# A two-layer graph network: GpSimd's gathers of layer 1's edges moved behind layer 0's scatters of tokens

## The chip, the core and the metric

The kernel runs on one core of a Trainium2 chip. The core has five engines with a queue each: TensorE (PE; its weight loads are shown as PEld), VectorE (DVE), ScalarE (ACT), GpSimd (POOL) and SyncE (SP). They run side by side and meet in semaphores. DMAs are issued from the queues of SP, ACT and POOL; the indirect ones, whose addresses come from a tile in SBUF, all from POOL. The metric is the time of one execution on the device in microseconds (us), as a median of several.

## The reference

Nodes: 3125 with 256 features; edges: 100,000, sorted by destination, each with one of 8 types. Two layers, each made of a graph part, an attention part and a mixture of experts:

```python
edge_index = jnp.stack([src, dst])
xn = _layernorm(x, axis=-1)
x = x + _L0_gnn_ref(xn, edge_index, ...) + _L0_mix_ref(xn[None], ...)[0]
x = x + _L0_ffn_ref(_layernorm(x, axis=-1)[None], ...)[0]      # 8 experts, top 2, hidden 1024, exact GELU
xn = _layernorm(x, axis=-1)
x = x + _L1_gnn_ref(xn, ..., edge_index, edge_type_8) + _L1_mix_ref(xn[None], ...)[0]
x = x + _L1_ffn_ref(_layernorm(x, axis=-1)[None], ...)[0]      # 6 experts, top 2
```

`_L0_gnn_ref` sums the neighbours of each node twice, with a linear layer, a norm and a SiLU after each sum. `_L0_ffn_ref` sends each node (a token) to the two of its 8 experts with the highest router probability. `_L1_gnn_ref` is an attention over the edges: a score for each edge from its source, destination and type, a softmax over the edges of a destination, and a weighted sum of the source rows.

## The kernel before, in words

128 partitions; the nodes stand in 25 blocks (NB) of 128. The stages, in order of time:

1. Layer 0's graph part builds a dense matrix of edge counts (adj) and sums neighbours as matrix products (L2183), twice. The second pass runs over groups of node columns, `GROUPS1`: five of 512, two of 256 and one of 128. After each group `Routes.tokens` works out, on VectorE, the router's choice for its blocks and where each token goes (`slot`, L1905), and POOL scatters the tokens, one indirect DMA for each block and each of the two choices (L1909, 50 in all), into the DRAM tensor `route_x`, sorted by expert. Then `Routes.plan` works out which tiles of which experts are left to do.
2. `Blocks` prepares layer 1's edges: the edges, sorted by destination, are cut into 25 blocks of 128 runs, with 34 edges a run (15 in the last block). Its constructor issues 75 indirect gathers on POOL (L1048): for each of dst, src and type, and each block, 128 runs of 34 whole numbers (136 bytes). `Blocks.finish` is a generator with the arithmetic on them, in pieces.
3. `Routes.results` works out from which row each token's result will come back, and writes it over `slot` (L1971); so it waits for the scatters that read the old `slot`.
4. `experts` runs 32 steps: 8 with the first 256 tokens of each expert, then 24 as the plan says. A step: SP loads its tokens `fx` from `route_x` (L1993), its weights (two of 1 MB, L2002 and L2004) and small rows; TensorE transposes the tokens (L2013), VectorE scales them into `fxe` (L2015); 8 times, a product of `fxe` with a part of the first weights goes to `fhp` (L2030, two buffers in PSUM) and ScalarE's GELU brings it to `fhid` (L2031); then 16 products with the second weights (L2038) give `fyp`, VectorE adds a row (L2040), and ACT's queue stores it (L2041). The next step's transposes stand between a step's fhp and fyp. After each step `beside(s)` is called: from step 8 on it advances `Blocks.finish` by a piece (the first reads `b_dst`, L1061), at step 16 POOL loads layer 1's weights `wn` (L2244, 8 DMAs), at step 22 `score_weights` multiplies them (L2064).
5. Layer 1: results are gathered back (L2300), the table of source rows is made (L2319), and for each block the rows of its edges are gathered by POOL (L1383, 831 gathers of 128 rows) and reduced by TensorE (L1468), with the attention's softmax, the six experts and small products for the scores (L1214, L1415, L1429) woven in.

The order of the work: outside the parts named next a scheduler places the instructions on each queue, by readiness and priority. In `with tc.manual_schedule(engines=ORDERED)` around `experts`, PE, DVE and ACT keep the order in which the code names the instructions; POOL and SP do not. A POOL instruction placed early in the queue is executed early, and what stands behind it waits. In the queue that was built, the 75 gathers and the 50 scatters are interleaved at the end: 44 scatters, 14 gathers of b_dst, 4 scatters, 11 gathers of b_dst, 6 of b_src, 2 scatters, 19 of b_src, 25 of b_rel (the types), 8 loads of wn. The first gather waits for a VectorE instruction of the second pass (L2195) and for counts of TensorE and ScalarE; each POOL DMA also waits for the one eight places before it.

Of the kernel before, what the change touches and what calls it, by code (L numbers as in the profile page):

```python
# [9 lines left out]
I32 = mybir.dt.int32  # L10
# [7 lines left out]
P = 128  # L18
# [390 lines left out]
def run_all(steps):  # L409
    for _ in steps:  # L410
        pass
# [493 lines left out]
BO = [sum(BW[:b]) for b in range(NB + 1)]  # L905
# [124 lines left out]
class Blocks:  # L1030
# [3 lines left out]
    def __init__(self, nc, keep, dram, pool, a, places):  # L1034
        k = lambda shape, dt, name: keep.tile(shape, dt, name=name)
        t = lambda shape, dt, name: pool.tile(shape, dt, name=name)
        n = BO[NB]
        self.at = k([P, n], I32, "b_at")
        self.dl = k([P, n], F32, "b_dl")
        self.rel = k([P, n], BF, "b_rel")  # L1040
        self.found = k([P, 1], F32, "b_found")
        self.order = dram.tile([n, P], BF, name="b_order")
        self.raw = raw = {}
        for name, src in (("dst", "dst"), ("src", "src"), ("rel", "edge_type_8")):
            raw[name] = t([P, n], I32, "b_" + name)
            flat = a[src].rearrange("(e o) -> e o", o=1)
            for b in range(NB):
                nc.gpsimd.indirect_dma_start(  # L1048
                    out=raw[name][:, BO[b]:BO[b + 1]], out_offset=None, in_=flat,
                    in_offset=bass.IndirectOffsetOnAxis(ap=places.blocks[:, b:b + 1], axis=0))  # L1050

    def finish(self, nc, C, dram, pool, ps):

# [81 lines left out]
class Layer1:  # L1135
# [50 lines left out]
    def load(self, A, c):  # L1186

        if c >= A["n"]:
            return
        k = min(CW, A["w"] - c * CW)  # L1190
        i = A["c0"] + c * CW
        oe = self.wk.tile([P, CW * P], BF, name="oe", bufs=3)
        self.nc.sync.dma_start(oe[:, :k * P], self.B.order[i:i + k, :].rearrange("c e -> (c e)")[None, :]
                               .to_broadcast([P, k * P]))
        A["oe"][c] = oe
# [849 lines left out]
def score_weights(nc, C, a, late, f, wn, blk_p):  # L2045

    at_w = f.tile([P, 2, 2 * HD], F32, name="at_w")
    head = f.tile([P, 2, HD], F32, name="head")
    for oc in range(2):
        nc.vector.tensor_scalar(head[:, oc, :], C.row[:, :HD], float(-4 * oc), C.pd[DH],  # L2050
                                op0=OP.add, op1=OP.is_equal)
    for i, name in enumerate(("L1_gnn_attn_srcc", "L1_gnn_attn_dstc")):
        col = f.tile([P, 2], F32, name=f"att{i}")
        nc.sync.dma_start(col, a[name])
        for oc in range(2):
            nc.vector.tensor_scalar(at_w[:, oc, i * HD:(i + 1) * HD], head[:, oc, :],
                                    col[:, oc:oc + 1], None, op0=OP.mult)

    score_w = late.tile([P, 2, 2 * R * HD], F32, name="score_w")
    sp = blk_p.tile([P, 2, R, 2 * HD], F32, name="sp", tag="w")  # L2060
    for r in range(R):
        for k in range(2):
            for oc in range(2):
                nc.tensor.matmul(sp[:, k, r, :], wn[:, r, oc, k * P:(k + 1) * P], at_w[:, oc, :],  # L2064
                                 start=(oc == 0), stop=(oc == 1))
    for k in range(2):
        nc.vector.tensor_copy(score_w[:, k, :R * HD].rearrange("p (r h) -> p r h", r=R),
                              sp[:, k, :, :HD])
        nc.vector.tensor_copy(score_w[:, k, R * HD:].rearrange("p (h r) -> p r h", r=R),
                              sp[:, k, :, HD:])  # L2070
    return score_w
# [3 lines left out]
def fast(ctx: ExitStack, tc: tile.TileContext, a, out, flag):  # L2075
    nc = tc.nc
# [28 lines left out]
    with tc.tile_pool(name="a_sb", bufs=1) as a_sb, tc.tile_pool(name="a_ps", bufs=2, space=PSUM) as a_ps, \  # L2105
# [3 lines left out]
        with tc.tile_pool(name="find", bufs=1) as find:  # L2109
            places = Places(nc, C, keep, find, a_ps, a)  # L2110
# [34 lines left out]
    with tc.tile_pool(name="g", bufs=1) as g1, tc.tile_pool(name="ga", bufs=4) as ga, \  # L2145
# [12 lines left out]
        for layer, parts in enumerate((px, py)):  # L2158
# [5 lines left out]
            for c, cw in (GROUPS if layer == 0 else GROUPS1):  # L2164
# [3 lines left out]
                for kb in range(NB // KB):  # L2168
# [9 lines left out]
                    for i in range(KB):  # L2178
                        k = k0 + i
                        n = P if k < NB - 1 else LAST  # L2180
# [31 lines left out]
                for i in range(nt):  # L2212
                    t = c // P + i
# [18 lines left out]
    with tc.tile_pool(name="blk", bufs=1) as blk, tc.tile_pool(name="blk_p", bufs=1, space=PSUM) as blk_p, \  # L2232
            tc.tile_pool(name="f", bufs=1) as f:
        B_ = Blocks(nc, late, dram, blk, a, places)

        score_w = None
        wn = f.tile([P, R, 2, D], F32, name="wn")
        steps = B_.finish(nc, C, dram, blk, blk_p)

        def beside(s):  # L2240
            nonlocal score_w
            if s == 16:
                for r in range(R):
                    nc.gpsimd.dma_start(wn[:, r], a["L1_gnn_W"][r].rearrange("(k p) n -> p k n", p=P))  # L2244
            if s == 22:
                score_w = score_weights(nc, C, a, late, f, wn, blk_p)
            if s >= 8:
                next(steps, None)
            if s < NE0 + NT - 1:
                return  # L2250
            run_all(steps)

            ok = blk.tile([P, 1], F32, name="ok")
            nc.vector.memset(ok, 1.0)
            tot = blk_p.tile([1, 1], F32, name="tot", tag="w")
            nc.tensor.matmul(tot, found_w, ok, start=True, stop=False)
            nc.tensor.matmul(tot, B_.found, ok, start=False, stop=True)
            nc.vector.tensor_scalar(flag, tot, float(2 * E), None, op0=OP.not_equal)

        T_.results(nc, C, blk)  # L2260
        with tc.tile_pool(name="fw", bufs=2) as fw, tc.tile_pool(name="fk", bufs=3) as fk, \
                tc.tile_pool(name="fp", bufs=2, space=PSUM) as fp:
            with tc.manual_schedule(engines=ORDERED):
                experts(tc, C, T_, a, f, fw, fk, fp, beside)


    with tc.tile_pool(name="n1", bufs=1) as n1:
# [7 lines left out]
        with tc.tile_pool(name="r", bufs=1) as r1, tc.tile_pool(name="rw", bufs=3) as rw, \  # L2275
# [21 lines left out]
            for t in range(NB):  # L2297
                for i in range(2):
                    y = rw.tile([P, D], F32, name=f"y{i}")
                    nc.gpsimd.indirect_dma_start(  # L2300
                        out=y, out_offset=None, in_=T_.y,
                        in_offset=bass.IndirectOffsetOnAxis(ap=T_.back[:, i * NB + t:i * NB + t + 1], axis=0))
# [22 lines left out]
                ap = rp.tile([P, 2 * R * HD], F32, name="ap", tag="b")  # L2325
# [8 lines left out]
                n = P if t < NB - 1 else LAST  # L2334
# [34 lines left out]
@with_exitstack  # L2369
def gps_two_layers(ctx: ExitStack, tc: tile.TileContext, a, out):  # L2370
    nc = tc.nc
    hold = ctx.enter_context(tc.tile_pool(name="hold", bufs=1))
    flag = hold.tile([1, 1], I32, name="flag")
    fast(tc, a, out, flag)
    with tc.If(nc.values_load(flag[0:1, 0:1], min_val=0, max_val=1) > 0):
        general(tc, a, out)
# [51 lines left out]
```

## Time and profile before

| | us |
|---|---|
| median of 3 runs | 3694.38 (3680.18 to 3694.63) |
| the profiled execution | 3702.6 |
| its span, first to last instruction | 3700.7 |
| first scatter of tokens (L1909) | 739.9 |
| first gather of b_dst (L1048) | 939.7 |
| last scatter of tokens, start | 985.8 |
| last gather of b_rel, start | 1041.5 |
| first fhp of the experts (L2030) | 1015.4 |
| end of the experts' last fyp | 1526.7 |
| first gather of results for layer 1 (L2300) | 1530.2 |

Busy over the whole span: PE 2658.4 us (72%), DVE 1753.3 (47%), ACT 735.2 (20%), POOL 1057.7 (29%). These shares are averages over stages with different limits, and say little of the stretch around the change. Between 950 and 1053 us PE was busy for 15.40 us, DVE 13.46, ACT 5.53 and POOL 76.37; between 1053 and 1500 us, in the experts' steps, PE for 445.04 of 447.

Such a profile is read from the end: the chain of waits follows the work that ended last back to what released it, step by step; "issue" in it is time in which an engine waited for nothing that the profile shows, and "remote" or "another core or an unknown queue" time whose releaser was not found. The timeline lists the instructions of each engine with the idle time before each.

### The profile page before, as it was taken

The page shows a single profiled execution, that of the slowest core. Times are in us where ns is not written, and L with a number is a line of the kernel's source. Part 1 is how long each engine was busy: PE and PEld are TensorE (multiplying, and loading weights), DVE is VectorE, ACT ScalarE, POOL GpSimd, SP SyncE. Part 2 cuts the span into 40 slices and gives each one's busy share as a digit, 9 for nine tenths or more (in the row PEclk, how much of TensorE's full clock was granted, in tenths as well). Part 3 has the DMA queues.
Part 4 walks back from the last instruction along what each step waited for, and adds up shares of the span by engine and source line. Part 5 has one row for each costly group of instructions (what it writes and reads, how often), then busy time and mean ns, then how long its engine had stood idle before and what let it go on. Part 6 is the DMA issues. An engine that isn't in the chain of part 4 may idle for free.

```text
span 3700.7 us, 38218 instructions
## 1 busy us (share of the span) xinstructions
PE 2658.4 (72%) x13696; PEld 1789.8 (48%) x13696; DVE 1753.3 (47%) x3882; ACT 735.2 (20%) x1637; POOL 1057.7 (29%) x1040
## 2 busy tenths in 40 slices
PE   2787999999179999799634527736655755755778
PEld 1565544546158888544323424534443543543456
DVE  6888533556301111376415545445454453554552
ACT  3344111212112222232100001102101111201122
POOL 1000000021620000320233554553554554554410
PEclk9899999999589999899867767877876877977899
DMA  8533222332346665553423332432342343343322
GB/s 298 152 79 74 84 77 66 89 118 72 86 132 192 192 197 161 152 158 122 138 78 85 96 108 78 116 113 78 104 121 82 98 120 92 98 121 91 96 65 81
DMA packets 382414, 421.68 MB, mean 114 GB/s; under 512 B 143878, under 2 KB 316044, under 8 KB 381958
## 3 DMA queue, kind: packets, MB, share of 16 engines
q1 hardware_dynamic: 311680, 270.61, 24.2%
q0 software_dynamic: 49072, 132.49, 12.8%
q10 hardware_dynamic: 21462, 16.03, 1.4%
q8 instruction: 110, 1.80, 0.2%
q14 instruction: 90, 0.74, 0.1%
HBM read 321.04 MB, written 97.96 MB: 113 GB/s over the span
## 4 chain that ended last, share of the span: by engine, by line
PE 55%; another core or an unknown queue 19%; DVE 14%; issue 4%; DMA 3%; ACT 2%; POOL 2%; ACTq 1%; SPq 0%; POOLq 0%; DVEq 0%
PE agg L2183 11%; PE fhp L2030 6%; PE fyp L2038 6%; PE sums L1468 6%; PE hp L1270 5%; PE hp L2319 4%; PE yp L1322 3%; DVE r L1454 2%; PE hp L2203 1%; DVE oh_a L1619 1%; DVE oh_s L1619 1%; PE kv L1727 1%; PE cnt L1634 1%; PE kvp L2337 1%
## 5 line engine op out<-in xcount | busy, mean ns | idle before, releaser
L1383 POOL DMA_INDIRECT r<-tab,b_at x831 | 863.2, 1039 | 1063.0 <-PE tp L1524 482.5
L1468 PE MATMUL sums<-r,oh 128*128 128x264 f32 x1662 | 435.7, 419 | 74.3 <-DVE oh L1457 55.8
L1214 PE MATMUL dp<-a,ot 128*128 128x64 bf16 x2493 | 116.6, 210 | 482.7 <-DVE own L1225 318.7
L1468 PEld LDWEIGHTS sums<-r,oh 128*128 128x128 f32 x1662 | 343.1, 209 | 161.6 <-issue 60.1
L1214 PEld LDWEIGHTS <-ot 128*128 128x128 bf16 x2493 | 108.6, 109 | 511.0 <-issue 398.6
L1909 POOL DMA_INDIRECT route_x<-x,slot x50 | 50.4, 1007 | 829.3 <-DVE slot L1905 678.2
L2030 PE MATMUL fhp<-fxe,fw 128*128 128x256 f32 x1024 | 238.7, 391 | 46.0 <-issue 20.6
L1225 DVE TENSOR_TENSOR own<-dp,orel 128x512 f32<-128x512 f32 (+1 forms) x122 | 74.1, 607 | 404.0 <-remote 313.1
L1454 DVE TENSOR_TENSOR r<-r 128x1792 f32<-128x1792 f32 (+2 forms) x123 | 240.5, 1955 | 0.0
L2183 PE MATMUL agg<-at,px 128*128 128x512 bf16 (+2 forms) x1050 | 237.5, 357 | 2.2 <-DMA row_g<-in_L_gnn_g 2.2
L1322 PE MATMUL yp<-ew,h 128*128 128x256 f32 x600 | 168.7, 433 | 95.9 <-DVE xs L1326 91.9
L2030 PEld LDWEIGHTS fhp<-fxe,fw 128*128 128x128 f32 x1024 | 189.3, 194 | 89.1 <-issue 23.6
L1273 ACT ACTIVATE h<-hp,bc 128x512 f32<-128x512 f32 (+2 forms) x168 | 105.2, 639 | 631.3 <-PE hp L1270 324.3
L2038 PE MATMUL fyp<-fw,fhid 128*128 128x256 f32 x1024 | 227.8, 381 | 0.0
L2183 PE MATMUL agg<-at,py 128*128 128x512 bf16 (+4 forms) x1200 | 218.7, 335 | 1.5 <-issue 1.5
L2038 PEld LDWEIGHTS fyp<-fw,fhid 128*128 128x128 f32 x1024 | 193.3, 191 | 25.3
L2300 POOL DMA_INDIRECT y<-route_y,slot x50 | 49.8, 996 | 510.6 <-DMA wq<-in_L_mix_wqT 481.8
L2319 PE MATMUL hp<-wt,xt 128*128 128x512 f32 x400 | 186.9, 615 | 11.7 <-ACT xt L345 3.1
L1322 PEld LDWEIGHTS yp<-ew,h 128*128 128x128 f32 x600 | 125.2, 218 | 133.4 <-DVE xs L1326 101.2
L2031 ACT ACTIVATE fhid<-fhp,fb 128x256 f32<-128x256 f32 x256 | 121.3, 474 | 323.2 <-PE fhp L2030 280.0
L1270 PE MATMUL hp<-xt,ew 128*128 128x512 f32 (+2 forms) x336 | 170.3, 629 | 19.2 <-ACT h L1273 12.2
L1270 PE MATMUL hp<-h,ew 128*128 128x512 f32 (+2 forms) x336 | 155.8, 590 | 2.1 <-issue 2.0
(418 smaller groups left out, 3810.5 us busy)
## 6 DMA issues: line engine op xcount, KB each, us to landing
fw<-in_L_ffn_W SPq DMA_DIRECT2D x64, 1024.0 KB
ew<-in_L_ffn_expert_w SPq DMA_DIRECT2D x126, 256.0 KB
at<-adj SPq DMA_DIRECT2D x44, 640.0 KB
route_x<-zero SPq DMA_DIRECT2D x104, 256.0 KB
tab<-stage SPq DMA_DIRECT2D x25, 1056.0 KB
oe<-b_order SPq DMA_DIRECT2D x97, 256.0 KB
adj<-adj_o SPq DMA_DIRECT2D x78, 250.0 KB
r<-tab,b_at POOLq DMA_INDIRECT x831
```

Source lines behind the costliest of these rows:

```text
L1214: nc.tensor.matmul(dp[:, i, :, :].rearrange("p h r -> p (h r)"), ot[:, i * P:(i + 1) * P], A["a3"][:, j, :], start=(j == 0), stop=(j == 2))
L1270: nc.tensor.matmul(hp[:, :W], ws[i, e][:, n, j * P:(j + 1) * P], x[:, n, :W], start=(n == 0), stop=(n == 1))
L1273: nc.scalar.activation(o[:, j, :W], hp[:, :W], AF.Relu, bias=b[:, e, j:j + 1])
L1322: nc.tensor.matmul(yp, h2[e][:, n, i * P:(i + 1) * P], ws[3, e][:, n, :], start=(n == 0), stop=(n == 1))
L1383: st = self.nc.gpsimd.indirect_dma_start(out=r[:, c, :], out_offset=None, in_=self.table, in_offset=bass.IndirectOffsetOnAxis(ap=self.B.at ...
L1454: nc.vector.tensor_tensor(rv, rv, r[:, :k, D:, None].to_broadcast([P, k, HD, DH]), OP.mult)
L1468: mm = nc.tensor.matmul(self.sums, oh[:, c, :], r[:, c, :], start=(i == 0), stop=(i == w - 1))
L2030: nc.tensor.matmul(hp, w1[:, k, i * P:(i + 1) * P], xe[:, k, :], start=(k == 0), stop=(k == 1))
L2031: nc.scalar.activation(hid[:, i, :], hp, AF.Gelu, bias=b1[:, 0, i:i + 1])
L2038: nc.tensor.matmul(yp, hid[:, i, t * P:(t + 1) * P], w2[:, i, :], start=(i == 0), stop=(i == K1 - 1))
L2183: nc.tensor.matmul(agg[g][:, :cw], parts[j][:n, k, g * P:(g + 1) * P], at[:n, i, :cw], start=(k == 0 and j == 0), stop=(k == NB - 1 and j ...
L2319: nc.tensor.matmul(hp.rearrange("p r d -> p (r d)"), xt[:, k, :], wt[:, k, j * 512:(j + 1) * 512], start=(k == 0), stop=(k == 1))
```

## The change

The gathers leave the constructor of `Blocks` and become a generator, `load`, that issues them five at a time under `keep_in_program_order`; `beside` advances it by two pieces after each of the steps 0 to 7. The loads of `wn` get `keep_in_program_order` too. The first pieces are thus named in the code after the scatters, and after the experts' step 0. `keep_in_program_order` fixes where an instruction stands in its queue; it adds no wait for another engine.

```diff
-        self.raw = raw = {}
+        self.raw = {name: t([P, n], I32, "b_" + name) for name in ("dst", "src", "rel")}
+        self.places = places
+
+    def load(self, tc, a):
+
         for name, src in (("dst", "dst"), ("src", "src"), ("rel", "edge_type_8")):
-            raw[name] = t([P, n], I32, "b_" + name)
             flat = a[src].rearrange("(e o) -> e o", o=1)
             for b in range(NB):
-                nc.gpsimd.indirect_dma_start(
-                    out=raw[name][:, BO[b]:BO[b + 1]], out_offset=None, in_=flat,
-                    in_offset=bass.IndirectOffsetOnAxis(ap=places.blocks[:, b:b + 1], axis=0))
+                tc.keep_in_program_order(tc.nc.gpsimd.indirect_dma_start(
+                    out=self.raw[name][:, BO[b]:BO[b + 1]], out_offset=None, in_=flat,
+                    in_offset=bass.IndirectOffsetOnAxis(ap=self.places.blocks[:, b:b + 1], axis=0)))
+                if b % 5 == 4:
+                    yield
...
+        loads = B_.load(tc, a)
         steps = B_.finish(nc, C, dram, blk, blk_p)
...
             if s == 16:
                 for r in range(R):
-                    nc.gpsimd.dma_start(wn[:, r], a["L1_gnn_W"][r].rearrange("(k p) n -> p k n", p=P))
+                    tc.keep_in_program_order(nc.gpsimd.dma_start(
+                        wn[:, r], a["L1_gnn_W"][r].rearrange("(k p) n -> p k n", p=P)))
...
-            if s >= 8:
+            if s < 8:
+                for _ in range(2):
+                    next(loads, None)
+            else:
                 next(steps, None)
```

In the queue that is built from it POOL has the 50 scatters, then the 25 gathers of b_dst, 25 of b_src, 25 of b_rel, then the 8 loads of wn. The other queues keep their order.

## The prediction

> **What bounds the kernel now.** I read the chain of waits first, for the stretch from the last aggregation of layer 0 to the second step of the experts (columns: start, length, what).
>
> ```profile
> 939.70 0.99 POOL b_dst L1048
> ...
> 956.25 0.94 POOL b_dst L1048
> 957.50 1.00 POOL route_x L1909
> ...
> 985.83 1.57 POOL route_x L1909
> 987.70 0.99 POOL b_src L1048
> ...
> 1010.26 2.25 DMA b_src<-in_src,bstart_i
> 1013.41 1.93 DVE fxe L2015
> 1015.38 1.22 PE fhp L2030 x2
> ...
> 1024.94 10.01 issue
> 1035.43 10.03 issue
> 1045.93 7.22 another core or an unknown queue
> ```
>
> From 939.70 to 1010 the end hangs on GpSimd's gathers. Thirty-one of them (14, then 11 and 6) stand ahead of the last six scatters of tokens, and the experts cannot load a token before the last scatter has landed. From 1024.94 on the chain shows something else: waits of ten microseconds that nothing in the profile explains.
>
> The timeline gives the two costs of the queue (the bracket is the idle time before the instruction and what ended it).
>
> ```profile
> 947.55 0.16 DVE L1905 CAST slot<-route_at 128x2 int32<-128x2 f32 x1
> 957.50 1.00 POOL L1909 DMA_INDIRECT route_x<-x,slot  x1 [0.30 <-issue]
> 978.25 0.15 DVE L1905 CAST slot<-route_at 128x1 int32<-128x1 f32 x1 [1.22 <-DVE pl_ci L1924]
> 985.83 1.57 POOL L1909 DMA_INDIRECT route_x<-x,slot  x1 [0.31 <-issue]
> 991.78 4.37 SPq L1993 DMA_DIRECT2D fx<-route_x  x4
> ```
>
> The slots of the seventh group are ready at 947.55 and its first scatter goes at 957.50: ten microseconds of pure queue. The last slots come at 978.25. Their VectorE chain is not long; it has become slow.
>
> The same view of ScalarE shows what slows it, with a normal step of the experts and a place in layer 1 beside it.
>
> ```profile
> 1020.06 0.85 ACT L2031 ACTIVATE fhid<-fhp,fb 128x256 f32<-128x256 f32 x2
> 1024.47 0.47 ACT L2031 ACTIVATE fhid<-fhp,fb 128x256 f32<-128x256 f32 x1 [3.56 <-PE fhp L2030]
> 1034.95 0.47 ACT L2031 ACTIVATE fhid<-fhp,fb 128x256 f32<-128x256 f32 x1 [10.01 <-issue]
> 1045.45 0.47 ACT L2031 ACTIVATE fhid<-fhp,fb 128x256 f32<-128x256 f32 x1 [10.03 <-issue]
> 1053.17 0.84 ACT L2031 ACTIVATE fhid<-fhp,fb 128x256 f32<-128x256 f32 x2 [7.24 <-remote]
> ...
> 1111.59 0.47 ACT L2031 ACTIVATE fhid<-fhp,fb 128x256 f32<-128x256 f32 x1 [0.39 <-PE fhp L2030]
> ```
> ```profile
> 2064.63 0.36 ACT L1417 COPY ls<-lp 8x256 f32<-8x256 f32 x1 [21.54 <-remote]
> 2091.40 0.17 ACT L1430 COPY sc<-cp 128x8 f32<-128x8 f32 x1 [26.41 <-remote]
> ```
>
> A GELU (L2031) normally follows its matmuls after 0.39 us; here it waits 10, although the matmuls before it ended at 1023.2 and 1026.1. In layer 1 the matmuls of cp (L1429) end at 2066.5 and ScalarE takes them at 2091.40. Both stand in an unbroken run of GpSimd's indirect DMAs: 939.70 to 1048.33 (with the eight loads of wn at its end), and 2041.0 to 2087.0. Both end 4 to 5 us after the run. So I read: **while GpSimd issues indirect DMAs without a pause, hand-overs between engines become late, those from TensorE worst, until about 4.8 us after the run.** The VectorE chain from 954.63 is the milder form: steps that took 0.2 us before it take 0.7 to 1.4.
>
> **The change, part by part.** *Removed from the front of the queue:* 31 gathers at 1.25 us (start to start, 939.70 to 975.19 for the b_dst). *Added:* no instruction. In the built program's GpSimd queue the 50 scatters now come first, then 75 gathers in one row, then the eight loads of wn. The gathers wait only for the DMA eight places before them and, once, for TensorE and ScalarE counts passed long ago: nothing ties a piece to its step. TensorE, VectorE, ScalarE and SP keep their order; only the lane that SP's first fx load waits for, and two of VectorE's waits on lanes, change.
>
> *When the last scatter goes.* With four scatters from 947.7 to 952.8 the queue then pauses. The VectorE chain stands at 954.63; six dependent steps of 0.2 us bring own (L1892) to 955.9. In the seventh group own to the second cast took 3.3 us (944.95 to 948.26), here one token block less: 3.0, so 959, with the first cast 0.7 earlier. Two scatters at 1.28 end at 960.6, against 987.4: **26.8 us earlier**.
>
> *When the experts start.* Scatter end to fx load 4.4 us (987.4 to 991.78): 965.0. Load to transposes 2.9 (994.66): 967.9. Transposes 1.1, fxe 1.0, to the first fhp 1.4 (1013.94 to 1015.38): 971.4. To the first GELU 4.7 (1020.06): **976.1, or 44 us earlier**. Before, fxe also stood behind the plan's slot cast (L1971, 1012.55); its chain of some 22 small steps starts here at 957.4 in an unslowed VectorE, and at 0.2 to 0.6 us each is done by 967, under the load.
>
> [...]
>
> *What is moved, and when it ends.* The run now starts at 960.9: 75 times 1.25 is 93.8, to 1054.7; the loads of wn took 5.9 (1042.45 to 1048.33), to 1060.5; plus 4.8 (1048.33 to 1053.17): engines are free again at **1065.3, not 1053.17: 12.1 us later**. Who needs these data is far off: b_dst at 1180.5 (L1061, step 8), wn at 1382.6 (L2064); GpSimd's next work is at 1530. This is covered by over 100 us; uncovered, VectorE would hold up fxe by the same amount.
>
> *The stretch between,* 976.1 to 1065.3, is 89 us inside the run; the trace has only 33 us of such a stretch (1020.06 to 1053.17), five GELUs long. By its rows: two GELUs at once, the third after 4.4, then one in 10.5. That gives the eighth GELU of step 0 at 980.5 + 5 x 10.5 = 1033.0. fyp starts 0.6 later and takes 8.4: 1042. The next fhp ends at 1043, two GELUs at 10.5 come by 1064, the third and fourth at 1065.3 and 1066.2. In the present trace step 1's fourth GELU starts at 1068.58. So **the gain is 2.4 us**. If the first 20 us of a run are clean (in layer 1 the first late hand-over comes at 2060, 19 us after 2041.0), GELUs three and four come by 978.5, 12.5 us sooner, and step 1's fifth comes with the release against 1069.45: a gain of 3.3. I take 3.
>
> Bounds of this unknown. *No late hand-over at all:* eighth GELU at 976.1 + 7 x 0.87 (1110.73 to 1111.59) = 982.2 against 1055.81: 73.6 us gained. *Stuck until the release, as at 2066:* two more GELUs at 1065.3, four at 0.87, the eighth at 1069.2 against 1055.81: 13.4 us lost.
>
> [...]
>
> The sum: 3702.6 (span 3700.7 and 1.9 around it) minus 3 is 3699.6; the profiled execution lies 8.2 above the median 3694.38, which gives **3691**.
>
> **Rivals.** *The brake is weak on the experts* (0.20). VectorE's hand-overs inside the run cost about 1.2 us; if TensorE's cost that, a GELU takes 0.87 + 1.2, a step 8 x 2.07 + 6.9 = 23.5. In 89 us that is 3.8 steps where now one is done: 2.8 x 14.35 (fhp at 1065.00 and 1079.35) is 40 gained, 3654. For: the hand-overs at 967.4 and 1020 were prompt. Against: all four after 1022, and layer 1. *No brake* (0.07): 3621; no long run in the trace speaks for it. *Stuck* (0.18): place, step 0's GELUs; price 13.4 (3708); it decides when fewer than six of them pass before the run ends, for then the later release is not paid back. For: 2066 to 2091. Against: the present gathers, of 136 bytes a row, let one through in 10.5. That the pieces do not run beside the steps, as the change says, is part of the forecast.
>
> **How the numbers follow.** The forecast has 0.55; its own range is 3680 to 3705, the spread of the runs (14 us) about it. To hold 0.8 the range takes in the stuck case whole and the upper half of the weak one: 3649 to 3708. No change, within 0.5% (18.5 us, about what a measurement of this kernel can tell), is most of the forecast, the stuck case where nothing lengthens it, and the near edge of the weak one: 0.62. Faster: weak and free, and a little of the forecast: 0.28. Slower: stuck with a run that is itself longer beside the experts' 2 MB of weights a step: 0.10.
>
> **What would show it.** The last scatter at about 959 and the first fhp at 971; 75 gathers without a gap to 1055; release at 1065; between, GELUs with idle times of 10 us and 10 to 14 of them in all; full steps of 14.35 afterwards, and layer 1 unchanged. I am wrong if GELUs run at under 3 us apiece inside the run, if the gathers stretch beyond 1070, or if the last scatter still waits past 970.

## The result, and the profile after

| | before | after |
|---|---|---|
| median of 21 runs, us | 3691.22 (3667.04 to 3709.52) | 3691.08 (3675.86 to 3705.59) |
| the profiled execution | 3702.6 | 3687.65 |
| its span | 3700.7 | 3685.6 |
| last scatter of tokens, end | 987.4 | 960.1 |
| first GELU of the experts | 1020.06 | 972.50 |
| end of the wn loads, and of GpSimd's run | 1048.33 | 1059.78 |
| step 1's eighth GELU | 1072.04 | 1074.74 |
| first gather of results, after the experts | 1530.16 | 1529.56 |

The ratio after to before is 1.0008 (95% interval 0.9992 to 1.0023): no difference. The two profiled executions differ by 15 us, but the experts end 0.6 us apart; the rest lies in layer 1, whose code is the same (2170.5 us from the first gather of results to the end before, 2156.0 after; a second profile of the kernel after has 2166.1). The profile of after runs 2.25 us ahead of that of before already at the seventh group's own (942.70 against 944.95), for reasons that lie before the change; where it matters this is said below. Lines of after are 5 higher than those of before up to the experts, 6 at wn, 10 from the gathers of results on; the gathers of edges, L1048 before, are L1051.

The chain of waits of after, for the stretch that was shown of before (start, length, what):

```profile
958.27 6.01 DMA route_x<-x,slot
...
965.03 2.96 DMA fx<-route_x
...
969.45 46.25 another core or an unknown queue
...
1016.72 43.78 another core or an unknown queue
1060.53 0.42 DVE fy L2045
1060.95 4.62 another core or an unknown queue
1065.58 0.41 DVE fy L2045
1066.01 0.43 ACTq L2046
1066.54 0.48 ACT fhid L2036
```

The gathers are gone from the front of the chain: from the last scatter it goes straight to the first load of tokens. In their place stand three waits without a known releaser, 94.7 us together, up to 1065.58. The timeline shows what they are (in brackets the idle time before an instruction and what ended it).

```profile
956.40 0.15 DVE L1910 CAST slot<-route_at 128x1 int32<-128x1 f32 x1
958.27 1.84 POOL L1914 DMA_INDIRECT route_x<-x,slot  x1 [0.30 <-DVE pl_ex L1945]
1052.95 0.95 POOL L1051 DMA_INDIRECT b_rel<-in_edge_type,bstart_i  x1 [0.30 <-issue]
1053.89 5.89 POOL L2250 DMA_DIRECT2D wn<-in_L_gnn_W  x8
964.30 1.62 SPq L1998 DMA_DIRECT2D fx<-route_x  x3
972.50 0.84 ACT L2036 ACTIVATE fhid<-fhp,fb 128x256 f32<-128x256 f32 x2
974.20 0.47 ACT L2036 ACTIVATE fhid<-fhp,fb 128x256 f32<-128x256 f32 x1 [0.86 <-issue]
...
984.92 0.47 ACT L2036 ACTIVATE fhid<-fhp,fb 128x256 f32<-128x256 f32 x1 [4.43 <-remote]
987.32 1.06 PE L2018 MATMUL ftp<-ident,fx 128*128 128x128 f32 x4
993.33 0.48 ACT L2036 ACTIVATE fhid<-fhp,fb 128x256 f32<-128x256 f32 x1 [7.93 <-remote]
1004.52 0.47 ACT L2036 ACTIVATE fhid<-fhp,fb 128x256 f32<-128x256 f32 x1 [10.72 <-remote]
1066.01 0.43 ACTq L2046 DMA_DIRECT2D route_y<-fy  x1
1066.54 0.84 ACT L2036 ACTIVATE fhid<-fhp,fb 128x256 f32<-128x256 f32 x2 [61.54 <-DVE fy L2045]
...
1005.05 5.98 PE L2043 MATMUL fyp<-fw,fhid 128*128 128x256 f32 x15 [10.50 <-issue]
1039.51 0.58 PE L2035 MATMUL fhp<-fxe,fw 128*128 128x256 f32 x1 [2.22 <-issue]
1067.07 7.64 PE L2035 MATMUL fhp<-fxe,fw 128*128 128x256 f32 x24 [26.98 <-ACT fhid L2036]
1015.73 0.99 DVE L2020 TENSOR_SCALAR fxe<-ftp,flng,flnb 128x256 f32<-128x256 f32 x2 [46.27 <-remote]
1060.53 0.42 DVE L2045 TENSOR_TENSOR fy<-fyp,fb 128x256 f32<-128x256 f32 x1 [43.80 <-remote]
```

Read it by engine. GpSimd issues 75 gathers without a gap from 960.42 to 1053.9, and wn to 1059.78. ScalarE's GELUs start promptly, then fall behind: 4, 8, 11 us. The eighth of step 0 passes at 1004.52. VectorE's next work, fxe of step 1, comes at 1015.73, 27 us after the transposes (ftp) that it reads ended at 988.38. TensorE has made the first half of fyp, 16 of its 32 matmuls, by 1011 at the latest. VectorE takes it at 1060.53, **some 50 us late**, the last 43.8 of them idle; the chain has 0.02 us between the signal that it waited for and its start, so what came late is the signal, and not VectorE. ScalarE's queue stands behind the store of that fy, and TensorE, which has crept through eight single matmuls of step 1, waits for ScalarE from 1040.1 on. Everything goes on between 1065.6 and 1066.5, some 6 us after GpSimd's last DMA was issued.

Not only what waits for another engine is slow. Those eight matmuls start 2.1 to 2.8 us apart, each after idle time in which TensorE waited for nothing that the profile shows ("issue"); at full pace a matmul of that line takes 0.22 us (before has 32 in 7.16 us from 1064.84).

Layer 1 has the same two rows as before, with 18.54 us of idle time for ls (21.54 before) and 26.33 for sc (26.41), in its run of gathers:

```profile
2059.86 0.36 ACT L1422 COPY ls<-lp 8x256 f32<-8x256 f32 x1 [18.54 <-remote]
2086.55 0.17 ACT L1435 COPY sc<-cp 128x8 f32<-128x8 f32 x1 [26.33 <-remote]
```

Idle time is not all lateness: the matmuls that ls reads ended at 2057.1, 2.7 us before it; those of sc at 2061.7, 24.9 us before it.

### The profile page after: what moved, and what is told of

It reads as the page before. It is cut to its first block, busy times and chain, and to the rows that moved or that the text cites. A ratio compares the mean times of both kernels' runs of the same rounds, so it can differ in the third digit from the quotient of the medians.

```text
span 3685.6 us, 38218 instructions
## 1 busy us (share of the span) xinstructions
PE 2660.9 (72%) x13696; PEld 1791.3 (49%) x13696; DVE 1750.9 (48%) x3882; ACT 734.8 (20%) x1637; POOL 1052.7 (29%) x1040
## 4 chain that ended last, share of the span: by engine, by line
PE 51%; another core or an unknown queue 21%; DVE 16%; issue 5%; DMA 3%; ACT 2%; POOL 1%; SPq 1%; ACTq 0%; DVEq 0%; POOLq 0%
PE agg L2188 10%; PE fhp L2035 6%; PE fyp L2043 6%; PE sums L1473 5%; PE hp L1275 4%; PE hp L2329 4%; PE yp L1327 3%; DVE r L1459 2%; PE hp L2208 1%; DVE oh L1462 1%; DVE oh_a L1624 1%; DVE oh_s L1624 1%; PE cnt L1639 1%; PE kv L1732 1%
```

## The experiments

The theory (T): an unbroken run of GpSimd's gathers holds up hand-overs between engines (the signal of one engine that another waits for) until it ends; the change brings the experts forward, gives the run to their first steps, and ends it later. Rivals: the experts start slowly by themselves (R1); the DMA engines' bandwidth is shared (R2); each gather costs its share wherever it stands (R3). Times below are medians beside runs of the kernel before on the same chip. This turned out to matter: on the four chips on which the experiments ran, the kernel before took 3685.82 (e1 to e4), 3116.69 (e5 to e8), 3692.58 (e9, e10) and 3118.68 us (e11, e12).

### Tying the pieces to their steps: e1_tied

```diff
+                if b % 5 == 0:
+                    at = self.pool.tile([P, 5], I32, name="b_tie", bufs=2)
+                    tc.nc.vector.tensor_copy(at, self.places.blocks[:, b:b + 5])
-                    in_offset=bass.IndirectOffsetOnAxis(ap=self.places.blocks[:, b:b + 1], axis=0)))
+                    in_offset=bass.IndirectOffsetOnAxis(ap=at[:, b % 5:b % 5 + 1], axis=0)))
```

> Edit on the kernel after: each piece of five gathers takes its offsets from a copy that VectorE makes behind the step's last row addition, so that ten gathers go beside each of the steps 0 to 7 and GpSimd pauses between them. Theory T (an unbroken run of GpSimd's gathers holds up the hand-overs between engines, more the longer it lasts): ten gathers are a run of 12.5 us, in which, by the trace of before, hand-overs are late by nothing in the first 10 us and by 0.9 to 8 us after; step 1's eighth GELU comes at about 993 (972.5 + 7 x 0.87 + 14.35) where the kernel after has 1074.74; each step may lose 0 to 4 us; 3616 to 3641 us. Rival R1 (the first steps of the experts are slow by themselves, whatever GpSimd does): 3686 to 3695. Rival R3 (each gather costs its share, 80/75 = 1.1 us, wherever it stands beside the experts): 3686 to 3695, with the first eight steps longer by 10 us each.

Measured: 3628.28 us beside 3685.82 (0.9843, 0.9808 to 0.9877), as T says. The same 75 gathers, at the same rate (1.25 us from start to start), in runs of ten beside steps 1 to 8; the timeline has GpSimd and ScalarE around the end of the first run of ten:

```profile
996.75 0.95 POOL L1054 DMA_INDIRECT b_dst<-in_dst,b_tie  x1 [0.30 <-issue]
1000.69 0.94 POOL L1054 DMA_INDIRECT b_dst<-in_dst,b_tie  x1 [2.99 <-DVE b_tie L1053]
1000.37 0.43 ACTq L2049 DMA_DIRECT2D route_y<-fy  x1
1015.59 0.43 ACTq L2049 DMA_DIRECT2D route_y<-fy  x1
```

A pause of 3 us after 12.5 us of gathers was enough here. The stores of two steps stand 15.22 us apart, where undisturbed steps have 14.30 (1106.06 to 1120.37): some 0.9 us a step, where one long run held two steps for 94 us. R1 and R3 fall.

### Moving the gathers to where GpSimd is idle: e2_early

The gathers go in fifteen pieces beside layer 0's edge counts, each behind a small copy on ScalarE, by way of DRAM.

```diff
             for g in range(NG):
...
                 counts.count(g)
+                if g % 5 == 1:
+                    next(loads, None)
...
+                    raw = wk.tile([P, BO[5]], I32, name="b_raw", bufs=2)
+                    at = wk.tile([P, 5], I32, name="b_tie", bufs=2)
+                    tc.nc.scalar.copy(at, places.blocks[:, b:b + 5])
...
+                    tc.nc.sync.dma_start(rawd[name][:, c0:BO[b + 1]], raw[:, :BO[b + 1] - c0])
```

> Edit on the kernel after: the 75 gathers go in fifteen pieces of five beside the edge counts, about 70 to 740 us, each piece behind a small copy on ScalarE; the pieces are stored to DRAM and loaded again for the blocks. Behind the scatters GpSimd has only the eight loads of wn (5.9 us). T: step 0's eighth GELU at 979 and step 1's at about 993, against 1074.74 in the kernel after: a gain of 75 to 82 us, 3609 to 3621 us; pieces of five last 6 us and hold up nothing. R1 (the experts' start is slow by itself): gain under 6, 3685 to 3695. R3 (each gather costs its share wherever it stands): the cost comes back in the edge counts, 3685 to 3695.

Measured: 3611.28 us (0.9807, 0.9758 to 0.9855), 74.5 less than before. The experts' first steps in its timeline:

```profile
956.86 5.92 POOL L2261 DMA_DIRECT2D wn<-in_L_gnn_W  x8
973.49 0.84 ACT L2044 ACTIVATE fhid<-fhp,fb 128x256 f32<-128x256 f32 x2
979.50 0.47 ACT L2044 ACTIVATE fhid<-fhp,fb 128x256 f32<-128x256 f32 x1 [0.39 <-PE fhp L2043]
987.30 0.44 ACTq L2054 DMA_DIRECT2D route_y<-fy  x1
993.86 0.47 ACT L2044 ACTIVATE fhid<-fhp,fb 128x256 f32<-128x256 f32 x1 [0.39 <-PE fhp L2043]
```

Eight GELUs in 6.5 us, step 1's eighth at 993.86 against 1074.74: the experts are not slow at their start.

### The run again, in the middle of the experts: e3_more, e4_direct

```diff
+            if s == 12:
+                tie = blk.tile([P, NB], I32, name="b_tie12")
+                nc.vector.tensor_copy(tie, places.blocks)
+                dum = [blk.tile([P, BO[NB]], I32, name=f"b_dum{j}") for j in range(3)]
+                for i in range(75):
+                    b = i % NB
+                    tc.keep_in_program_order(nc.gpsimd.indirect_dma_start(
+                        out=dum[i // NB][:, BO[b]:BO[b + 1]], out_offset=None,
+                        in_=a["dst"].rearrange("(e o) -> e o", o=1),
+                        in_offset=bass.IndirectOffsetOnAxis(ap=tie[:, b:b + 1], axis=0)))
```

In e4_direct the body is a `dma_start` of 128 x 34 numbers, and a write of VectorE into the first target ties it to step 12.

> Edit on e2_early: 75 further gathers of the same kind, into tiles that nobody reads, in one row behind step 12 of the experts, where the steps run at 14.35 us. T: a run of 94 us in which hand-overs from TensorE are late; from the kernel after, whose run held two steps' work in the 94 us from 972.5 to 1066.5: 65 to 90 us longer than e2_early. R1: 0 to 5 us longer. R2 (what is lost is bandwidth of the DMA engines: 1.28 MB more, where a step moves 2 MB in 14.35 us): 0 to 9 us longer.

> Edit on e2_early: the same as e3_more with 75 direct DMAs of the same shape (128 rows of 136 bytes) from GpSimd's queue in place of the indirect ones. T as far as it says that indirect DMAs do it: 0 to 6 us longer than e2_early. T in its wide form (any unbroken run of DMAs from GpSimd): 65 to 90 us longer. R2 (bandwidth): 0 to 9 us longer, the same as e3_more.

Measured: e3_more 3707.44 us (1.0060, 1.0036 to 1.0084), **96.2 over e2_early**, somewhat more than expected; e4_direct 3606.89 (0.9802, 0.9771 to 0.9833), no different from e2_early. The timeline of e3_more:

```profile
1158.33 0.99 POOL L2265 DMA_INDIRECT b_dum<-in_dst,b_tie  x1 [201.03 <-ACT fhid L2044]
1251.69 5.90 POOL L2271 DMA_DIRECT2D wn<-in_L_gnn_W  x8
1163.85 0.47 ACT L2044 ACTIVATE fhid<-fhp,fb 128x256 f32<-128x256 f32 x1 [0.39 <-issue]
1196.74 0.37 ACTq L2054 DMA_DIRECT2D route_y<-fy  x1
1211.31 0.47 ACT L2044 ACTIVATE fhid<-fhp,fb 128x256 f32<-128x256 f32 x1 [10.55 <-remote]
1222.20 0.47 ACT L2044 ACTIVATE fhid<-fhp,fb 128x256 f32<-128x256 f32 x1 [10.41 <-remote]
1263.51 0.84 ACT L2044 ACTIVATE fhid<-fhp,fb 128x256 f32<-128x256 f32 x2 [7.95 <-remote]
```

Steps that ran at full pace break down within one step of the run's start: the next store comes at 1196.74 instead of some 1172, then one GELU in 10 or 11 us, and all is well 6 us after the last wn (1257.6). Nothing reads what these gathers bring, and e4_direct moves the same bytes: R1 and R2 fall for good. That direct DMAs are harmless as such isn't shown: in e4_direct GpSimd waited for its own transfers after every 1 to 11 of them, by 0.4 to 2.4 us, so its run was never unbroken.

### A shorter run: e5_short and e10_short, and the kernel after again

```diff
+                at = self.places.blocks
+                if name == "rel":
+                    if b % 5 == 0:
+                        tie = self.pool.tile([P, NB], I32, name="b_tie", bufs=2)
+                        tc.nc.vector.tensor_copy(tie[:, b:b + 5], at[:, b:b + 5])
+                    at = tie
```

with the offsets taken from `at`: the last 25 gathers, and wn behind them, leave the run.

> Edit on the kernel after: the 25 gathers of b_rel, with the loads of wn behind them, leave the run: each piece of five waits for a VectorE copy of its offsets behind the row additions of steps 5, 6 and 7; the 50 gathers of b_dst and b_src stay in one row. T (the end of the run sets the time): the run ends at 960.4 + 50 x 1.25 = 1023 instead of 1059.8, 37 us sooner; engines are free at about 1028 instead of 1066; less 1 us for each of the three steps with ten gathers: 32 to 38 us faster than the kernel after, 3653 to 3659 us beside an after of 3691, that is 0.989 to 0.993 of before. R1 (slow start of the experts, whatever GpSimd does): 0.998 to 1.001. R3 (each gather its 1.1 us): 0.998 to 1.001.

Measured: 3094.17 us beside a kernel before of 3116.69 (0.9915, 0.9886 to 0.9945). The ratio is what T gave, but not for T's reason: no run held up anything here. That is best seen in e8_store, which is the kernel after but for one store and ran on the same chip. Its run of 75 gathers is the one of after, and beside it the GELUs of steps 0 and 1 come every 0.87 us (timeline):

```profile
1052.92 0.94 POOL L1051 DMA_INDIRECT b_rel<-in_edge_type,bstart_i  x1 [0.30 <-issue]
978.43 0.47 ACT L2036 ACTIVATE fhid<-fhp,fb 128x256 f32<-128x256 f32 x1 [0.39 <-PE fhp L2035]
...
992.68 0.47 ACT L2036 ACTIVATE fhid<-fhp,fb 128x256 f32<-128x256 f32 x1 [0.39 <-PE fhp L2035]
```

The shares of the chain of waits over the whole span, after first:

```profile
PE 51%; another core or an unknown queue 21%; DVE 16%; issue 5%; DMA 3%; ACT 2%; POOL 1%; SPq 1%; ACTq 0%; DVEq 0%; POOLq 0%
```

and e8_store:

```profile
PE 64%; DVE 16%; DMA 7%; POOL 6%; issue 5%; ACT 2%; SPq 1%; ACTq 0%; DVEq 0%; POOLq 0%
```

The waits without a releaser, 21% of 3685.6 us, are gone. Layer 1 shows it too: ScalarE's 25 copies sc (L1435) stood idle behind "remote" for 205.1 us in after, and in e8_store for 40.5 us in all, each until its own matmuls ended. It isn't TensorE's clock: the mean granted clock is 0.917 there and 0.856 in after, but TensorE's busy time is 2594.9 against 2660.9 us, 66 of the 584 us between the spans. So the theory had to be narrowed to T2, and the kernel after itself and the program of e5_short ran once more.

> The kernel after itself. The three kernels e5_short to e7_twenty ran where the kernel before takes 3117 us instead of 3686 and where GELUs inside the run stood 0.39 us behind their matmuls: no hand-over was late. Theory T2 (the hold-up of a run belongs to some chips and not to others; without it the change brings the 27 us of its earlier scatters, with it it gives them back): where before takes 3117 us, after is 18 to 27 us faster, 0.991 to 0.994 of before, and GELUs in the run come every 0.87 us; where before takes 3690 us, 0.998 to 1.002. Rival R1 (the gain is lost in the experts' slow start): 0.998 to 1.002 on either.

> The same program as e5_short (the gathers of b_rel tied to steps 5 to 7, wn behind them), beside the kernel after on one chip. T2: where before takes 3690 us, the run ends at 1023 instead of 1060 and the kernel is 32 to 38 us faster than after; where before takes 3117 us there is nothing to be released from and it is within 5 us of after.

Measured, beside a kernel before of 3692.58: e9_after 3693.07 us (1.0003, 0.9982 to 1.0023), e10_short 3656.23 (0.9906, 0.9880 to 0.9932), 36.8 less than after. The timeline of e10_short:

```profile
1019.88 0.94 POOL L1057 DMA_INDIRECT b_src<-in_src,bstart_i  x1 [0.30 <-issue]
1029.58 0.43 ACTq L2052 DMA_DIRECT2D route_y<-fy  x1
1030.11 0.84 ACT L2042 ACTIVATE fhid<-fhp,fb 128x256 f32<-128x256 f32 x2 [29.65 <-DVE fy L2051]
1037.95 0.47 ACT L2042 ACTIVATE fhid<-fhp,fb 128x256 f32<-128x256 f32 x1 [0.39 <-PE fhp L2041]
```

The run ends at 1020.8 where that of e9_after ends, wn with it, at 1055.8: 35.0 us sooner. Step 1's first GELUs come at 1030.11 where e9_after has them at 1062.68, 32.6 us sooner. **The end of the run set the time here,** nearly one for one: 35.0 us sooner, 36.8 us less.

### What fell on chips without the hold-up: e6_gaps, e7_twenty, e8_store, e12_gaps, e11_late

e6_gaps and e12_gaps are one program: e3_more with a clear of a tile, three times, after every tenth gather. e7_twenty is e3_more with `range(20)`. e8_store is after with

```diff
-        nc.scalar.dma_start(T.y[s * TS:(s + 1) * TS, :].rearrange("(t p) d -> p t d", p=P), y)
+        nc.sync.dma_start(T.y[s * TS:(s + 1) * TS, :].rearrange("(t p) d -> p t d", p=P), y)
```

> Edit on e3_more (75 further gathers in one row behind step 12, 96 us over e2_early): after every ten of them GpSimd clears a tile of 831 numbers three times, an estimated 3 us by the iota rows (0.10 us for 1, 0.23 for 128 numbers), so that it issues nothing for a while but never waits. T (a pause in the issuing is enough, whatever GpSimd does in it): each run is 12.5 us as in e1_tied, whose steps took 15.28 instead of 14.30 us: about 1 us for each of 8 runs, 5 to 20 us over e2_early, 3616 to 3631 us. Rival R4 (GpSimd itself must stand at a wait for the others to go on): the run only grows by 7 x 3 us, 100 to 120 us over e2_early.

> Edit on e2_early: 20 further gathers in one row behind step 12 (e3_more has 75 and cost 96 us). In e3_more step 13's GELUs were still in time 5.5 us into the run and fy came only at 1196, 38 us into it. T (nothing in the first 10 us, then held up until the run of 25 us and the 5.9 us of wn behind it are over, about 36 us after its start): fy and the store of step 13 come at the end, some 20 us late: 12 to 24 us over e2_early, 3623 to 3635 us. Rival R5 (only runs beyond 30 us hold anything up): 0 to 5 us over e2_early.

> Edit on the kernel after: the store of a step's rows (route_y from fy) goes from SP's queue instead of ScalarE's, so that step 1's GELUs don't stand behind a store that waits for VectorE's fy. T: GELUs of step 1 pass inside the run, one in about 10 us from 1024 on, three or four of them before the release at 1066; its eighth comes at 1070 to 1072 instead of 1074.74: 2 to 5 us sooner. If the hand-over from TensorE to ScalarE is stuck as well, the eighth stays at 1073 to 1076.

> The same program as e6_gaps, whose first run fell where no hand-over is late; the three clears take 2.51 us together. Where before takes 3690 us: T (a pause in the issuing is enough, whatever GpSimd does in it), 5 to 25 us over e2_early, 0.981 to 0.988 of before; R4 (GpSimd itself must stand at a wait), 100 to 120 us over e2_early, 1.007 to 1.013 of before. Where before takes 3117 us: 0.992, as e6_gaps.

Measured: e6_gaps 3092.84 us (0.9922, 0.9898 to 0.9945), e7_twenty 3092.81 (0.9925, 0.9902 to 0.9947), both beside 3116.69; e12_gaps 3093.65 beside 3118.68 (0.9929, 0.9901 to 0.9958); e8_store, a single time, 3103.41 beside 3116.69. With 75 gathers behind step 12 in pieces, with 20 in one row, or (e5_short) with 75 beside the experts' first steps: 3092.8 to 3094.2 us. None of their questions is answered: they are about a hold-up that wasn't there.

e11_late is e2_early with the wn loads tied to step 16:

```diff
+                nc.vector.memset(wn[:, 0, 0, :1], 0.0)
                 for r in range(R):
```

> Edit on e2_early: the eight loads of wn wait for a VectorE write into their tile at step 16; in e2_early they stood behind the scatters, and the first tokens took 7.3 us from the issue of their load to the transposes (961.01 to 968.32) where e1_tied took 2.9 (961.62 to 964.49). T2 with shared bandwidth: the first transposes come 4.4 us sooner; where before takes 3690 us, 3604 to 3612 us or 0.977 to 0.980 of before; where it takes 3117 us, 3085 to 3095 or 0.989 to 0.993. Rival: the loads only move and take the same from step 17: no difference from e2_early.

Measured: 3098.25 us beside 3118.68 (0.9941, 0.9925 to 0.9958), a little above the 0.989 to 0.993 of T2. What moving wn brings can't be read from it: e6_gaps, e7_twenty and e12_gaps have wn behind the gathers of step 12 too, so no run on such a chip has the order of e2_early. The load itself answers: its first tokens took 2.8 us to the transposes (952.72 to 955.52), and 2.8 also in e3_more (963.73 to 966.49), which ran beside e2_early and has wn later too. So the 7.3 us of e2_early go with the wn loads.

## Why the prediction was right, point by point

**The total** was right, 3691 forecast and 3691.08 measured; that they agree to a tenth is luck, for before itself came to 3691.22 here where the forecast started from 3694.38. The reason was right too: what the earlier start brings, the later end of the run takes away. The experiments bear the reason out from three sides: without the run 74.5 us go (e2_early), a run elsewhere costs 96.2 (e3_more), and a run that ends 35.0 us sooner ends the kernel 36.8 us sooner (e10_short).

**The front of the queue** came as worked out: last scatter's end 960.1 (960.6 forecast), first load 964.30 (965.0), transposes 967.33 (967.9), first GELU 972.50 (976.1). With the 2.25 us by which this profile is ahead, the scatters were 1.8 us later than the step had them and the GELU 1.4 us sooner. From the last scatter's end to the first load were 4.2 us, where the step had 4.4.

**The run** ended at 1059.78 (1060.5), and engines were free between 1065.56 and 1066.54 (1065.3).

**The stretch between is the step that failed.** The prediction put step 0's eighth GELU at 1033.0, fyp's end at 1042, and four of step 1's GELUs at 1043 to 1066.2, for a gain of 2.4 us. Measured: the eighth GELU at 1004.52, since the first five came within 8 us; fyp's end at 1018; but then no GELU before 1066.54, since VectorE got fyp only at 1060.53 and ScalarE stood behind the store of fy. So eight GELUs passed in the run, where 10 to 14 were forecast. The price per hand-over was taken from GELUs alone, and those from TensorE to VectorE were costed at nothing: ftp to fxe took 27 us, and fyp to fy some 50. Step 1's fourth GELU came at 1070.89 against 1068.58 before: 2.3 us lost in place of 2.4 gained, and 4.6 lost if the 2.25 us are counted by which this profile was ahead; at the experts' end 0.6 gained, or 1.6 lost. Against the 89 us of the stretch all of these are small, since the release came at the time forecast, which is why the sum held.

**Two readings of rows** were off. The 0.39 us before a GELU, to which the prediction and the expectations compare late ones, is not the delay behind its matmuls: it is ScalarE's idle time between two GELUs, 0.87 us apart and 0.47 long. And of the 21.54 us before ls most is idle time with nothing to do: the matmuls that it reads ended at 2060.1, 4.5 us before it. The 24.9 us of sc and the 8.8 of a GELU (1026.1 to 1034.95) stand.

**The rivals.** *Weak* (3654) and *no brake* (3621) fall where before takes some 3690 us: only kernels with the run shortened (e10_short, 3656), broken up (e1_tied, 3628) or gone (e2_early, 3611) came to such times. *Stuck* by its own rule, fewer than six GELUs in the run, did not come true, as eight passed; but its mechanism did, one step on, from fy. That **the pieces don't run beside their steps** held: 75 gathers without a gap. Tied for good, as e1_tied ties them, they bring 57.5 us.

**What the prediction didn't know** is that its mechanism doesn't belong to the program alone. It took the free case as a rival with 0.07; on two of the four chips of the experiments it is what was seen. What the change brings there wasn't measured: the kernel after did not run on one. The nearest are e5_short, 22.5 us below before, and e8_store, 13.3 by its single time. Beside the same run in e8_store hand-overs are prompt: by its chain of waits fhp starts 0.04 us after fxe ends (968.93), and TensorE's next matmuls 0.04 us after a GELU ends (972.90).

**The best version** is e2_early: it is 74.5 us below before where gathers hold up hand-overs (and after equals before there). Where they don't, it did not run; its kin e11_late, e7_twenty and e12_gaps are 20 to 25 us below before.

## What to carry to other kernels

Here hand-overs that took ten microseconds and more, with "remote" or "issue" as releaser (10.03 us before a GELU of before, 43.80 before fy in after), stood in an unbroken run of GpSimd's indirect DMAs; where a trace shows the like, look for such a run around it. Reordering the run only moved the hold-up (3691.22 us before, 3691.08 after), and its end, not its start, set what followed (35.0 us sooner in e10_short, 36.8 us less). Breaking it helped in two forms: ten gathers and then a real wait of 3 us, tied to another engine's work by a dependency (e1_tied, 3628.28 us beside 3685.82), and the gathers in pieces where GpSimd is idle (e2_early, 3611.28). An order in the queue added no wait: in after 75 gathers went without a gap from 960.42 to 1053.9. Run the kernel on more than one chip before a mechanism is taken for a property of the program: the kernel before took some 3690 us on two of the four chips of the experiments, and 3117 on the others.

## What the runs showed of the hardware that was not expected

- The same kernel before takes 3685.82 and 3692.58 us on two chips and 3116.69 and 3118.68 on two others, 18% apart. The difference lies beside GpSimd's gathers: of the 584 us between the spans of after and e8_store 82 had come up by the first gather of results (1529.56 against 1447.50), and the other 502 in layer 1 with its 831 gathers. Whether it is the chip itself or something else that ran there at the time, these runs don't tell. Nor do they tell whether the hold-up is there when nothing is recorded: every time here has its span and clock from a recording of that execution.
- Inside such a run not every hand-over was late alike: in after, VectorE's fxe for step 1 came at 1015.73, 27 us late, and fy at 1060.53, some 50 us late, while TensorE issued single matmuls 2.8 us apart (1036.71, 1039.51).
- The load of the first tokens was slower beside other loads, and by less: in e2_early it took 7.3 us from its issue to the transposes (961.01 to 968.32), beside 2 MB of wn, and in e1_tied 2.9 us and in e3_more 2.8 without.
- Open stay: from which length a run holds up (ten gathers cost a step 0.9 us, 75 cost 96), whether GpSimd may compute in the pause instead of waiting, whether direct DMAs in an unbroken row do the same, what part the store in ScalarE's queue has, and by what way such a run holds up engines that don't wait for it. The runs made for the first, the second and the fourth fell on chips where there was nothing to see.
